# Seven products for eight in the A12 B21 term of gate and up, and table look-ups shared between VectorE and ScalarE

## The chip, the cores and the metric

The kernel runs on one core of one Trainium2 chip. The metric is the device time of that core in microseconds (us). Before the change three runs gave 1091.67, 1090.79 and 1091.09 us; their median is 1091.09 us. The core has a matrix engine (TensorE, PE in the profile; its weight loads are PEld), a vector engine (VectorE, DVE), an activation engine (ScalarE, ACT), a general engine (GpSimd, POOL), which here only issues transfers, and SyncE (SP), which issues most transfers. Each engine works through its own queue in order.

## What is computed

The input x has the shape 2 x 2048 x 512, float32. The reference is one pre-normed block of a transformer:

```python
x = x + attention(layernorm(x), Wq, Wk, Wv, Wo)
x = x + ffn(layernorm(x), lut, gate_idx, up_idx, down_idx)

def attention(x, Wq, Wk, Wv, Wo):      # between channels: 512 x 512 per batch element
    q, k, v = x @ Wq, x @ Wk, x @ Wv
    weights = softmax(q.T @ k / sqrt(16))
    return (weights @ v.T).T @ Wo

def ffn(x, lut, gate_idx, up_idx, down_idx):
    gate = x @ lut[gate_idx].T         # gate_idx, up_idx: 1376 x 512, values 0 to 15
    up = x @ lut[up_idx].T
    return (silu(gate) * up) @ lut[down_idx].T     # down_idx: 512 x 1376
```

The weights of the feed-forward part are not given as numbers but as indices into a table `lut` of 16 float32 values. So they have to be looked up, 3 x 1376 x 512 entries in all, before TensorE can use them.

## The kernel before the change

The 4096 tokens are handled as 8 chunks of 512 tokens (`NCH`), each of 4 blocks of 128 (`J`). The inner size 1376 is cut into 11 tiles of 128 rows, the last of 96 (`FT`, `NFT`). All products are in float32, in which one matmul of the code, 128x128 by 128x512, becomes two PE instructions in the profile. The program runs in stages, one after the other on TensorE:

- the Gram stage (`gram`, L427): normalizes x and multiplies it with itself for each batch element, block by block;
- the squares (`Square`, L580): small 512x512 products that turn the Gram matrix and the attention weights into one matrix m per batch element, with the softmax between them;
- the attention output (the loop at the end of which line 841 stands): for each of 32 blocks k it transposes a stored block on VectorE (`n_turned`, L734), multiplies it by m (`y_product`, L739), adds it to x and takes the statistics of the second layernorm (`added`, L747, with ScalarE doing a square and a sum), and normalizes the block six behind on ScalarE (`f_normed`, L757), which also issues a store of it every second block. The stored blocks are loaded again by GpSimd's queue and transposed by VectorE 16 blocks later;
- gate and up (`GateUp`, L860), in 44 units (f, p): tile f of the weights, pair p of chunks (1024 tokens);
- down (`Down`), with stores of the result.

Gate and up are multiplied together, by Strassen's scheme in Winograd's form: with gate weights A11, A12 on top and up weights A21, A22 below (A11 is two blocks of 128 wide along the contracted axis, and so are the others), and two chunks of tokens as B's columns, seven products replace eight. Each product of a unit is two matmuls, so a unit has 14. `Line.run` (L927) writes the order of a unit by hand: a1, c1, then the previous unit's last product a4, then a2, c2, b (which is A12 B21) and a3. After each of these seven stages it calls `between` (L962). The products a1, a2, a3 and a4 accumulate one after the other in one PSUM bank, and c1 and c2 in another. Between two of them ScalarE copies the intermediate sum out (p, p7 and u2, at L884, L890 and L895), VectorE adds (c2, b, a3), and ScalarE applies silu to the two halves of the result (h0 after b, h1 after a4). The next product into the bank has to wait for such a copy.

The look-ups are `Job`s (L236). A job fetches indices by a DMA from GpSimd's queue, ScalarE casts them to int16 (`cast`, L247), and VectorE does everything else (`ops`, L255): it makes three bit masks and one full-width mask out of the lowest bit, makes 8 choices between neighbouring table entries (L275), and then 7 choices by the other three bits with `copy_predicated` (L287). A gate-and-up job does both matrices of one f at once, 1024 entries per partition, followed by four sums for Strassen's scheme (`after`).

The look-ups have no place of their own: all jobs form one generator (`looked_up`, L350), and `pump(us)` (L367) draws operations from it where the hand-written order has room. Each operation yields a cost in us, and `pump` keeps what is owed:

```python
def pump(us):
    owed[0] = min(owed[0] + us, 2 * us + 1.0)
    while owed[0] > 0:
        cost = next(lookup, None)
        if cost is None:
            return
        owed[0] -= cost
```

A job whose gate is shut (its weight buffer is still in use) yields None; what is owed then stays. `between` pumps 1.0, or takes one operation out of the list `todo` in place of it. Line 841 pumps 1.4 for each of the first 16 blocks of the attention output and 0.7 for each of the others. In the Gram stage and the squares the pumps add up to 22.4 and 32.0.

Of the kernel before, what the change touches and what calls it, by code (L numbers as in the profile page):

```python
# [63 lines left out]
def tile_attn_ffn(  # L65
# [45 lines left out]
    eps_sb = const.tile([P, 1], F32, tag="eps", name="eps_sb")  # L111
    lut_i = lut_sb.bitcast(I32)
# [11 lines left out]
    wgu = tc.alloc_tile_pool(name="wgu", bufs=2)  # L124
# [111 lines left out]
    class Job:  # L236
        def __init__(self, name, rows, cols, load, dest, after, gate):
            self.name, self.rows, self.cols = name, rows, cols
            self.load, self.dest, self.after, self.gate = load, dest, after, gate

        def fetch(self, queue=nc.gpsimd):
            self.idx = gub.tile([P, 1024], I32, tag="idx", name=f"idx_{self.name}", bufs=2)[
                : self.rows, : self.cols
            ]
            self.load(queue, self.idx)
# [5 lines left out]
        def bits(self, tag, bufs):  # L251
            t = gub.tile([P, 1024], I16, tag=tag, name=f"{tag}_{self.name}", bufs=bufs)
            return t[: self.rows, : self.cols]

        def ops(self):  # L255

            rows, f, idx, b3 = self.rows, self.cols / 1024, self.idx, self.b3
            vec = nc.vector
            w = self.dest()
            b1, b2 = self.bits("b1", 1), self.bits("b2", 1)  # L260
            vec.tensor_scalar(b1, b3, 2, None, ALU.bitwise_and)
            vec.tensor_scalar(b2, b3, 4, None, ALU.bitwise_and)
            yield 0.2 + 0.54 * f

            vec.tensor_scalar(idx, idx, 31, 31, ALU.logical_shift_left, ALU.arith_shift_right)
            yield 0.1 + 0.55 * f
            vec.tensor_scalar(b3, b3, 8, None, ALU.bitwise_and)
            yield 0.1 + 0.27 * f
            masks = [None, b1, b2, b3]

            def pick(level, at, dest):

                if level == 1:
                    k = at // 2
                    vec.tensor_scalar(  # L275
                        dest.bitcast(I32), idx, lut_x[:rows, k : k + 1],
                        lut_i[:rows, at : at + 1], ALU.bitwise_and, ALU.bitwise_xor,
                    )
                    yield 0.2 + 0.55 * f
                    return  # L280
                yield from pick(level - 1, at, dest)
                half = 1 << (level - 1)
                t = gub.tile(
                    [P, 1024], F32, tag="pick", name=f"{self.name}_{level}_{at}", bufs=3
                )[:rows, : self.cols]
                yield from pick(level - 1, at + half, t)
                vec.copy_predicated(dest, masks[level - 1], t)  # L287
                yield 0.1 + 1.17 * f

            yield from pick(4, 0, w)  # L290
            yield from self.after()

    gu = {}
    passed = [0]

    def gu_job(f):
        f0, rows = FT[f]
        n = KB * rows

        def load(queue, idx):  # L300
            queue.dma_start(idx[:, :n], gate_idx[:, KB * f0 : KB * f0 + n])
            queue.dma_start(idx[:, n:], up_idx[:, KB * f0 : KB * f0 + n])

        def dest():
            gu[f] = {
                "w": wgu.tile([P, 2, KB, P], F32, tag="w", name=f"w_{f}"),
                "s": wgu.tile([P, 3, 2, P], F32, tag="s", name=f"s_{f}"),
            }
            flat = gu[f]["w"].rearrange("p g k r -> p (g k r)")[:, : 2 * n]
            gu[f]["flat"] = flat  # L310
            return flat

        def after():
            flat = gu[f]["flat"].rearrange("p (g k r) -> p g k r", g=2, k=KB)
            a11, a12 = flat[:, 0, 0:2, :], flat[:, 0, 2:4, :]
            a21, a22 = flat[:, 1, 0:2, :], flat[:, 1, 2:4, :]
            s1, s2, s4 = (gu[f]["s"][:, q, :, :rows] for q in range(3))
            for op, d, u, v in (
                (add, s1, a21, a22), (sub, s2, s1, a11), (sub, a21, a11, a21), (sub, s4, a12, s2)
            ):  # L320
                op(d, u, v)
                yield 0.42
            gu[f].update(
                {"11": a11, "12": a12, "S3": a21, "22": a22, "S1": s1, "S2": s2, "S4": s4}
            )

        return Job(f"gu{f}", P, 2 * n, load, dest, after, lambda: f < 2 + passed[0])

    def down_job(i, n=1):

        f0, rows = FT[i]

        def load(queue, idx):
            queue.dma_start(
                idx.rearrange("p (o e) -> p o e", o=n),
                down_idx[f0 : f0 + n * rows, :].rearrange("(o p) e -> p o e", o=n),
            )

        def dest():
            return wd[:rows, i : i + n, :].rearrange("p o e -> p (o e)")  # L340

        return Job(f"wd{i}", rows, n * E, load, dest, lambda: iter(()), lambda: True)


    jobs = [gu_job(0), gu_job(1), down_job(0, 2), down_job(2, 2), down_job(4), gu_job(2)]
    for i in range(5, NFT):
        jobs += [gu_job(i - 2), down_job(i)]
    jobs += [gu_job(f) for f in range(NFT - 2, NFT)]

    def looked_up():  # L350

        for i, job in enumerate(jobs):
# [4 lines left out]
            for k, cost in enumerate(job.ops()):  # L357
                yield cost
                if k == 9 and i + 1 < len(jobs):
                    jobs[i + 1].cast()  # L360
# [167 lines left out]
    for c in range(1, NCH):  # L528
        for j in range(J):
# [19 lines left out]
            if c == 1 and j == 2:  # L549
                nc.vector.tensor_tensor(  # L550
                    lut_x, lut_pairs[:, :, 0], lut_pairs[:, :, 1], ALU.bitwise_xor
                )
            if c == CPB and j == 1:
                gram_out(0)
# [274 lines left out]
    for k in range(NBLK):  # L829
# [11 lines left out]
        pump(1.4 if k < LAG else 0.7)  # L841
# [7 lines left out]
    def psum(tag, name):  # L849
        return fps.tile([P, E], F32, tag=tag, name=name, bufs=2)  # L850
# [8 lines left out]

    class GateUp:  # L860


        def __init__(self, f, p):
            self.f, self.p, self.rows = f, p, FT[f][1]
            self.name = f"{f}_{p}"

# [30 lines left out]
        def c2(self):  # L897
            mm(self.c, self.pairs("22", "T4"), False)
            self.c21 = self.temp("c21")
            add(self.c21, self.c, self.u2)  # L900

        def b(self):
            b = self.view("b")
            mm(b, self.pairs("12", "21"), True)
            self.h0 = self.temp("h0", 2)
            add(self.h0, b, self.p1)
            nc.scalar.activation(self.h0, self.h0, AF.Silu)  # L907
# [6 lines left out]
        def first(self):  # L914
            nc.vector.tensor_tensor(self.h0, self.h0, self.c21, ALU.mult)
            self.store(self.h0, 2 * self.p)

        def a4(self):
            mm(self.a, self.pairs("S4", "22"), False)
            self.h1 = self.temp("h1", 2)  # L920
# [6 lines left out]
    class Line:  # L927
# [5 lines left out]
        def run(self, u, final=False):  # L933
# [3 lines left out]
            self.between()  # L937
            last, self.last = self.last, u
# [4 lines left out]
            self.between()  # L943
            u.c2()
# [17 lines left out]
    def between():  # L962
        if todo:
            todo.pop(0)()
        else:
# [82 lines left out]
    class Down:  # L1048
# [94 lines left out]

        def end(self):
# [13 lines left out]
    for f, p in units:  # L1158
        while "S4" not in gu[f]:
            next(lookup)  # L1160
        assert p in xs
        if f == NFT - 1 and p == 0:
            assert not todo and next(lookup, None) is None
            xnp.release()
# [7 lines left out]
            todo += by_two(down_sums(hps["dT"]))  # L1172
# [6 lines left out]
        if p == NPR - 1:  # L1179
            passed[0] = f + 1  # L1180

# [83 lines left out]
```

## Time and profile before

| | us |
|---|---|
| median of three runs | 1091.09 |
| time of the profiled execution | 1091.32 |
| its span on the core | 1089.1 |
| TensorE busy | 1081.1 |
| VectorE busy | 712.3 |
| ScalarE busy | 321.4 |
| GpSimd busy | 33.4 |

The profile is of one execution. Its rows of slices cut the span into 40 equal parts of about 27 us, and each digit is the busy share of a slice in tenths. A row of a group of instructions names line, engine, operation, output and input, shape and count; behind the bar stand the total busy time in us, the mean of one in ns, and the idle time of the engine just before them with what ended it. "PE a_g L855" is a matmul of gate and up, in bank a. TensorE's granted clock was 1.00 in all the stretches looked at. The chain of work that ended last is TensorE for 92% of the span, ScalarE and VectorE for 3% each.

### The profile page before, as it was taken

Reading aid. Unit: us, or ns where it says so; the run is one execution under the profiler, and the core shown is the slowest. Engines: PE = TensorE matmul, PEld = TensorE weight load, DVE = VectorE, ACT = ScalarE, POOL = GpSimd, SP = SyncE. Lnnn points to the kernel's source line nnn. Section 1 sums busy time; section 2 is a strip of 40 time slices with the busy share of each in tenths; the row PEclk is TensorE's granted clock in tenths of the full one; section 3 lists DMA queues with packets and bytes.
Section 4 is the critical chain, followed back from the end, with each engine's and each line's share of the span. In section 5 each row is a group of like instructions: output and inputs, shape, how many; then the busy total and the mean of one; then the engine's idle time right before and its main releaser. Section 6 shows DMA issues by size and latency. Waiting matters only on the chain.

```text
span 1089.1 us, 10098 instructions
## 1 busy us (share of the span) xinstructions
PE 1081.1 (99%) x3458; PEld 647.9 (59%) x3458; DVE 712.3 (65%) x1357; ACT 321.4 (30%) x586; POOL 33.4 (3%) x66
## 2 busy tenths in 40 slices
PE   8999999999999999999999999999999999999998
PEld 5668886444444444444444444444338888888887
DVE  7878777887685787788878787763653334433341
ACT  4652532555622222222222222222222111111110
POOL 0000000112100000000000000000000000000000
PEclk9999999999999999999999999999999999999999
DMA  8650313697651111111121111111415554345421
GB/s 343 220 191 21 77 39 88 156 230 203 168 141 39 58 67 50 58 58 68 48 68 67 56 58 54 48 49 39 147 49 177 172 152 155 101 146 179 154 68 39
DMA packets 87699, 117.13 MB, mean 108 GB/s; under 512 B 14160, under 2 KB 50256, under 8 KB 86752
## 3 DMA queue, kind: packets, MB, share of 16 engines
q1 hardware_dynamic: 62784, 83.91, 24.4%
q0 software_dynamic: 4800, 15.80, 5.8%
q10 hardware_dynamic: 20064, 16.78, 4.8%
q8 instruction: 27, 0.44, 0.2%
q14 instruction: 24, 0.20, 0.1%
HBM read 68.76 MB, written 47.71 MB: 107 GB/s over the span
## 4 chain that ended last, share of the span: by engine, by line
PE 92%; ACT 3%; DVE 3%; ACTq 1%; DMA 1%; issue 1%; SPq 0%; DVEq 0%
PE a_g L855 28%; PE a_d L855 14%; PE c_g L855 14%; PE y L743 10%; PE c_d L855 7%; PE b_g L855 7%; PE b_d L855 4%; PE ea_t L580 1%; PE ea_p L580 1%; PE ea_m L580 1%; ACT xn_a L229 1%; PE gp L427 1%; ACT n L229 1%; DMA x<-in_x_dram 1%; DVE st_a L151 1%
## 5 line engine op out<-in xcount | busy, mean ns | idle before, releaser
L743 PE MATMUL y<-m,nT 128*128 128x512 f32 x256 | 110.2, 592 | 0.0
L133 DVE TENSOR_TENSOR c<-c_g,u 128x512 f32<-128x512 f32 (+1 forms) x44 | 30.4, 691 | 114.3 <-PE c_g L855 114.3
L743 PEld LDWEIGHTS y<-m,nT 128*128 128x128 f32 x256 | 48.6, 190 | 60.4 <-issue 58.6
L855 PE MATMUL c_g<-xb,w 128*128 128x512 f32 (+1 forms) x176 | 82.7, 592 | 0.0
L855 PE MATMUL a_g<-xT_a,s 128*128 128x512 f32 (+1 forms) x176 | 82.7, 592 | 0.0
L855 PE MATMUL a_g<-xb,w 128*128 128x512 f32 (+1 forms) x176 | 82.7, 592 | 0.0
L855 PE MATMUL b_g<-xb,w 128*128 128x512 f32 (+1 forms) x176 | 82.7, 592 | 0.0
L855 PE MATMUL a_g<-xb,s 128*128 128x512 f32 (+1 forms) x176 | 82.7, 592 | 0.0
L907 ACT ACTIVATE h<-h 128x512 f32<-128x512 f32 (+1 forms) x44 | 27.7, 630 | 163.2 <-DVE h L133 163.2
L427 PE MATMUL gp<-xn_a 128*128 128x128 f32 (+3 forms) x256 | 70.3, 435 | 2.7 <-DVE xn_a L174 1.6
L855 PE MATMUL a_g<-xT_sq,s 128*128 128x512 f32 (+1 forms) x132 | 62.0, 592 | 0.0
L427 PEld LDWEIGHTS gp<-xn_a 128*128 128x128 f32 x256 | 43.9, 190 | 29.6 <-issue 15.1
L275 DVE TENSOR_SCALAR gu<-idx_gu,lut_x,lut_sb 128x1024 int32<-128x1024 int32 (+1 forms) x77 | 58.4, 791 | 0.0
L855 PEld LDWEIGHTS a_g<-xb,s 128*128 128x128 f32 (+1 forms) x176 | 33.0, 188 | 42.6 <-issue 38.2
L855 PEld LDWEIGHTS a_g<-xT_a,s 128*128 128x128 f32 (+1 forms) x176 | 33.0, 188 | 42.5 <-issue 42.5
L855 PEld LDWEIGHTS b_g<-xb,w 128*128 128x128 f32 (+1 forms) x176 | 33.0, 188 | 42.5 <-issue 42.5
L855 PEld LDWEIGHTS c_g<-xb,w 128*128 128x128 f32 (+1 forms) x176 | 33.0, 188 | 42.5 <-issue 42.3
L855 PEld LDWEIGHTS a_g<-xb,w 128*128 128x128 f32 (+1 forms) x176 | 33.0, 188 | 42.5 <-issue 42.5
L287 DVE COPY_PREDICATED gu<-b_gu,gu 128x1024 f32<-128x1024 int16 (+1 forms) x44 | 56.4, 1281 | 0.8
L855 PE MATMUL a_d<-dT,hs_a 128*128 128x256 f32 x224 | 56.2, 378 | 0.0
L287 DVE COPY_PREDICATED wd<-b_wd,wd 128x512 f32<-128x512 int16 (+2 forms) x63 | 54.1, 859 | 1.1
L884 ACT COPY p<-a_g 128x512 f32<-128x512 f32 (+1 forms) x44 | 25.8, 586 | 78.0 <-PE a_g L855 78.0
(246 smaller groups left out, 1751.0 us busy)
## 6 DMA issues: line engine op xcount, KB each, us to landing
hd<-h SPq DMA_DIRECT2D x80, 256.0 KB, 2.0
h<-hd SPq DMA_DIRECT2D x40, 512.0 KB, 6.6
nl<-nd SPq DMA_DIRECT2D x32, 256.0 KB, 5.6
xnd<-xn_f ACTq DMA_DIRECT2D x16, 512.0 KB, 5.9
fl<-xnd POOLq DMA_DIRECT2D x32, 256.0 KB, 6.2
xn_back<-xnd SPq DMA_DIRECT2D x32, 256.0 KB, 3.7
out_dram<-r SPq DMA_DIRECT2D x31, 256.0 KB, 2.9
x<-in_x_dram SPq DMA_DIRECT2D x7, 1024.0 KB, 14.0
```

The source lines that it names most:

```text
L133: nc.vector.tensor_tensor(dest, a, b, ALU.add)
L151: nc.vector.bn_stats(st, block)
L229: nc.scalar.activation(to, block, AF.Identity, bias=self.nmr[:, j : j + 1], scale=self.rstd[:, j : j + 1],)
L275: vec.tensor_scalar(dest.bitcast(I32), idx, lut_x[:rows, k : k + 1], lut_i[:rows, at : at + 1], ALU.bitwise_and, ALU.bitwise_xor,)
L287: vec.copy_predicated(dest, masks[level - 1], t)
L427: nc.tensor.matmul(gp[b][i][:, i * P :], xn[:, i, j % 2, :], xn[:, i:, j % 2, :], start=c % CPB == 0 and j == 0, stop=c % CPB == CPB - 1 a ...
L580: nc.tensor.matmul(ps[:, m, :], self.a[a][:, k, m * P : (m + 1) * P], self.b[b][:, k, :], start=first and m == k == 0, stop=k == 1, skip_g ...
L743: nc.tensor.matmul(ys[k], nTs[k][:, i, :], m[:, i, :], start=(i == 0), stop=(i == KB - 1))
L855: nc.tensor.matmul(ps, lhsT, rhs, start=first and i == 0, stop=i == len(pairs) - 1, skip_group_check=not first,)
L884: nc.scalar.copy(self.p1, self.a)
L907: nc.scalar.activation(self.h0, self.h0, AF.Silu)
```

## The change

It has two parts.

**Products.** For f = 2 to 9, the four units made by two neighbouring f and two neighbouring p (a "group") share the term A12 B21. Seen over the group this is a product of 2x2 blocks, and it is done by the seven products of the same scheme, one matmul each, in place of eight. Each unit has a role, 0 to 3. Role 0 does two of the products, role 1 three (two of them in the new calls `extra1` and `extra2`, which come after c1 and after a2), role 2 two (one in `extra1`), role 3 none. They accumulate in two new single banks, x and y; two intermediate sums (r5, r6) are kept in SBUF by ScalarE copies. New sums of blocks are made on VectorE: `l2_sums` once per two pairs, `l2_left` for each two f. For f = 10 two blocks of B are already overwritten, so b uses two other sums there. c2's sum is now made in u2's place.

**Look-ups.** All jobs are 512 entries wide: gate and up are separate. The first six jobs of the list (`SHARED = 6`) are done by VectorE as before. In the other 27 the choice by the lowest bit is ScalarE's: b0 is 0 or 1, and an ACTIVATE with a per-partition scale and bias gives entry + b0 x (next entry - entry) for one 16-bit half of the table entry, as an integer, written to every second 16 bits of the result. So each of the 8 choices takes two ACTIVATEs, and no full-width mask is needed. The gates of the jobs change: a gate job may run up to 3 tiles ahead of the last f whose units have all been written out, an up job 2 tiles ahead of the last f whose a4 has been. The costs that the new job yields are written in the code below. The pumps of the attention output go from 1.4 and 0.7 to 1.6 and 1.0, and `between` pumps 0.3 beside an operation of `todo`.

```diff
...
         def ops(self):
+            return self.shared_ops() if self.scalar else self.vector_ops()
+
+        def shared_ops(self):
+
+
+            rows, f, b3 = self.rows, self.cols / 1024, self.b3
+            vec = nc.vector
+            w = self.dest()
+            b0, b1, b2 = self.bits("b0", 1), self.bits("b1", 1), self.bits("b2", 1)
+
+            def by_bit0(at, dest):
+                d = dest.bitcast(I16).rearrange("p (c h) -> p c h", h=2)
+                for h in range(2):
+                    nc.scalar.activation(
+                        d[:, :, h], b0, AF.Identity, bias=lut_h[:rows, at, h : h + 1],
+                        scale=lut_d[:rows, at // 2, h : h + 1],
+                    )
+
+            def temp(tag, bufs=1):
+                t = gub.tile([P, 512], F32, tag=tag, name=f"{tag}_{self.name}", bufs=bufs)
+                return t[:rows, : self.cols]
+
+            def both(mask, dest, t):
+                vec.copy_predicated(dest, mask, t)
+                return 0.15 + 1.17 * f
+
+            vec.tensor_scalar(b0, b3, 1, None, ALU.bitwise_and)
+            vec.tensor_scalar(b1, b3, 2, None, ALU.bitwise_and)
+            by_bit0(0, w)
+            t0 = temp("k1", 2)
+            by_bit0(2, t0)
+            yield 0.54
+            vec.tensor_scalar(b2, b3, 4, None, ALU.bitwise_and)
+            vec.tensor_scalar(b3, b3, 8, None, ALU.bitwise_and)
+            t4, t6 = temp("k2"), temp("k1", 2)
+            by_bit0(4, t4)
+            by_bit0(6, t6)
+            yield 0.54
+            t8 = temp("k3")
+            by_bit0(8, t8)
+            yield both(b1, w, t0)
+            t10 = temp("k1", 2)
+            by_bit0(10, t10)
+            yield both(b1, t4, t6)
+            yield both(b2, w, t4)
+            t12 = temp("k2")
+            by_bit0(12, t12)
+            t14 = temp("k1", 2)
+            by_bit0(14, t14)
+            yield both(b1, t8, t10)
+            yield both(b1, t12, t14)
+            yield both(b2, t8, t12)
+            yield both(b3, w, t8)
+            yield from self.after()
+
...
+        return Job(f"g{f}", P, n, load, dest, after, lambda: f < 3 + passed[0])
...
+        def after():
+            g, u = gw[f], up[0].rearrange("p (k r) -> p k r", k=KB)
+            t = wgu.tile([P, 3, 2, P], F32, tag="s", name=f"s_{f}", bufs=2)
+            a11, a12, a21, a22 = g[:, 0:2, :], g[:, 2:4, :], u[:, 0:2, :], u[:, 2:4, :]
+            s1, s2, s4 = (t[:, q, :, :rows] for q in range(3))
+            for op, d, v, w in (
                 (add, s1, a21, a22), (sub, s2, s1, a11), (sub, a21, a11, a21), (sub, s4, a12, s2)
             ):
-                op(d, u, v)
+                op(d, v, w)
                 yield 0.42
-            gu[f].update(
-                {"11": a11, "12": a12, "S3": a21, "22": a22, "S1": s1, "S2": s2, "S4": s4}
-            )
-
-        return Job(f"gu{f}", P, 2 * n, load, dest, after, lambda: f < 2 + passed[0])
-
-    def down_job(i, n=1):
-
+            gu[f] = {"11": a11, "12": a12, "S3": a21, "22": a22, "S1": s1, "S2": s2, "S4": s4}
+        return Job(f"u{f}", P, n, load, dest, after, lambda: f < 2 + ended[0])
...
+    SHARED = 6
+
+    jobs = [job(f) for f in range(2) for job in (gate_job, up_job)]
+    jobs += [down_job(i) for i in range(6)]
+    for f in range(2, NFT - 1, 2):
+        jobs += [gate_job(f), up_job(f), gate_job(f + 1), up_job(f + 1), down_job(5 + f // 2)]
+    jobs += [gate_job(NFT - 1), up_job(NFT - 1), down_job(NFT - 1)]
+    assert len(jobs) == 3 * NFT
+    for job in jobs[SHARED:]:
+        job.scalar = True
...
-                if k == 9 and i + 1 < len(jobs):
+                if k == (5 if job.scalar else 9) and i + 1 < len(jobs):
                     jobs[i + 1].cast()
...
-        pump(1.4 if k < LAG else 0.7)
+        pump(1.6 if k < LAG else 1.0)
...
+    def l2_sums(g):
+
+        x11, x21 = xb[4 * g][:, 2, :], xb[4 * g][:, 3, :]
+        x12, x22 = xb[4 * g + 2][:, 2, :], xb[4 * g + 2][:, 3, :]
+        t = x2p.tile([P, 3, CH], F32, tag=f"l{g}", name=f"l2b_{g}")
+        t1, t2, t4 = (t[:, q, :] for q in range(3))
+        l2b[g] = {"11": x11, "21": x21, "22": x22, "T1": t1, "T2": t2, "T3": x12, "T4": t4}
+        return [
+            lambda: sub(t1, x12, x11), lambda: sub(t2, x22, t1),
+            lambda: sub(x12, x22, x12), lambda: sub(t4, x21, t2),
+        ]
...
+        a11, a12 = gw[f][:, 2, :], gw[f][:, 3, :]
+        a21, a22 = gw[f + 1][:, 2, :], gw[f + 1][:, 3, :]
+        s1, s2, s3, s4 = (t[:, q, :] for q in range(4))
+        l2a[f // 2] = {"22": a22, "S1": s1, "S2": s2, "S3": s3, "S4": s4}
+        return [
+            lambda: add(s1, a21, a22), lambda: sub(s2, s1, a11),
+            lambda: sub(s3, a11, a21), lambda: sub(s4, a12, s2),
+        ]
...
+            self.role = 2 * (f % 2) + p % 2 if 1 < f < NFT - 1 else None
...
-            self.c21 = self.temp("c21")
-            add(self.c21, self.c, self.u2)
+            add(self.u2, self.c, self.u2)
+        def extra1(self):
+            if self.role == 1:
+                mm(two["x"], self.pair("S2", "T2"), False)
+                two["r6", self.p // 2] = r6 = self.kept("r6")
+                nc.scalar.copy(r6, two["x"])
+            elif self.role == 2:
+                two["y"] = self.view("y")
+                mm(two["y"], self.pair("S3", "T3"), True)
+                r5 = two["r5", self.p // 2]
+                add(r5, two["y"], r5)
+
+        def extra2(self):
+            if self.role == 1:
+                mm(two["x"], self.pair("S1", "T1"), False)
+                two["r5", self.p // 2] = r5 = self.kept("r5")
+                nc.scalar.copy(r5, two["x"])
...
+            elif self.role == 0:
+                two["x"] = self.view("x")
+                mm(two["x"], [(gw[self.f][:, 2, :], l2b[g]["11"])], True)
+                b = self.view("b")
+                mm(b, [(gw[self.f][:, 3, :], l2b[g]["21"])], True)
+                add(h0, two["x"], self.p1)
+                add(h0, b, h0)
+            elif self.role == 1:
+                mm(two["x"], self.pair("S4", "22"), False)
+                add(h0, two["x"], self.p1)
+            elif self.role == 2:
+                mm(two["y"], self.pair("22", "T4"), False)
+                add(h0, two["r6", g], self.p1)
+                add(h0, two["y"], h0)
+            else:
+                add(h0, two["r5", g], self.p1)
+            nc.scalar.activation(h0, h0, AF.Silu)
...
         def a4(self):
             mm(self.a, self.pairs("S4", "22"), False)
+            if self.p == NPR - 1:
+                ended[0] = self.f + 1
...
             u.c1()
             self.between()
+            u.extra1()
             last, self.last = self.last, u
             if last is not None:
                 last.a4()
                 self.between()
             u.a2()
             self.between()
+            u.extra2()
             u.c2()
...
     def between():
         if todo:
             todo.pop(0)()
+            pump(0.3)
         else:
             pump(1.0)
...
-        while "S4" not in gu[f]:
+        while f not in gu or f > 1 and min(f + 1, NFT - 1) not in whole:
             next(lookup)
         assert p in xs
+        if 1 < f < NFT - 1 and f % 2 == 0 and p == 0:
+            todo += l2_left(f)
...
+        if f == 1 and p % 2:
+            todo += l2_sums(p // 2)
```

## The prediction

> **What bounds the kernel now.** I read the page's busy shares and slices first, then busy times by stretch, the chain, the cost of single instructions, and ScalarE's (ACT's) timeline in one unit.
>
> ```profile
> span 1089.1 us, 10098 instructions
> PE 1081.1 (99%) x3458; PEld 647.9 (59%) x3458; DVE 712.3 (65%) x1357; ACT 321.4 (30%) x586; POOL 33.4 (3%) x66
> PE   8999999999999999999999999999999999999998
> DVE  7878777887685787788878787763653334433341
> ACT  4652532555622222222222222222222111111110
> ```
>
> TensorE (PE) never rests. VectorE (DVE) is at 7 to 8 tenths until slice 26, ACT at 2 in the gate-and-up stage but 5 to 6 in the stage before it (slices 7 to 10). Busy times of four stretches (the second to fifth figures are PE, PEld, DVE, ACT):
>
> ```profile
> 192.00:232.00 40.00, 40.00 (x94) 17.67 (x93) 33.30 (x82) 22.77 (x52) 5.59 (x10) 1.00 0.76 183
> 232.00:275.00 43.00, 43.00 (x102) 19.00 (x101) 33.73 (x84) 22.25 (x53) 7.66 (x14) 1.00 0.84 217
> 289.75:819.00 529.25, 529.25 (x1242) 232.58 (x1242) 389.30 (x618) 149.21 (x246) 15.07 (x28) 1.00 0.20 66
> 395.16:407.18 12.02, 12.02 (x30) 5.32 (x28) 10.59 (x14) 2.99 (x5) 1.08 (x2) 1.00 0.26 88
> ```
>
> The first two lie in the attention output ("y"), the third is all of gate and up, the fourth one unit (f, p) of it. The chain in that unit is PE alone:
>
> ```profile
> 395.32 1.72 PE c_g L855 x4
> 397.04 3.43 PE a_g L855 x8
> 400.48 1.72 PE c_g L855 x4
> 402.19 1.72 PE b_g L855 x4
> 403.91 3.43 PE a_g L855 x8
> ```
>
> A product of two 128-row blocks takes 1.72 us (four PE instructions), so one matmul of the code takes 0.86, and a unit 14 x 0.86 = 12.02. What ACT does meanwhile:
>
> ```profile
> 395.42 0.59 ACT L884 COPY p<-a_g 128x512 f32<-128x512 f32 x1 [0.89 <-PE a_g L855]
> 397.12 0.59 ACT L890 COPY p<-c_g 128x512 f32<-128x512 f32 x1 [1.12 <-PE c_g L855]
> 398.80 0.60 ACT L921 ACTIVATE h<-a_g 128x512 f32<-128x512 f32 x1 [1.09 <-PE a_g L855]
> 400.57 0.59 ACT L895 COPY u<-a_g 128x512 f32<-128x512 f32 x1 [1.17 <-PE a_g L855]
> 404.67 0.63 ACT L907 ACTIVATE h<-h 128x512 f32<-128x512 f32 x1 [3.52 <-DVE h L133]
> ```
>
> Each copy empties a bank that PE accumulates into again two stages (3.43 us) after it is filled. So a copy may start 3.43 - 0.59 = 2.8 us late; any later and PE stands.
>
> **The change, part by part.** *Products.* Units with f = 2 to 9 form 8 groups of four. A12 B21 costs a group's four units 2, 3, 2 and 0 matmuls, 7 for 8: 8 x 0.86 = **6.9 us less** on PE, all on the path. New sums on DVE: three adds of 0.68 per group, four 128-column sums per pair of f, eight 512-wide sums once: 8 x 2.0 + 4 x about 1 + 5.5 = 26 us; two ACT copies per group, 8 x 1.2 us.
>
> *Look-ups, DVE.* A 512-wide look-up costs DVE now (rows below) 8 x 0.54 + 7 x 0.73 + about 1.2 = 10.6 us, afterwards 7 x 0.73 + 4 x 0.28 = 6.2. Over 27 of them, most cheaper per entry now since 1024 wide, DVE loses some 80 us. That is worth nothing by itself: PE's waits on DVE add up to a few us in the trace. It does cover the new sums, VectorE's in-place sum into u2 and the moved table preparation (two small operations more), all costed at nothing (without it a unit's DVE, 10.6 of 12.0 us, would be nearly full). The u copy now also waits for the unit before it to have multiplied u2 away, 5 stages earlier: nothing, unless DVE lags by some 6 us (then the lag, at most). The index loads halve and double in number on POOL's queue, where they land 3 us after issue and are wanted about 7 us later: nothing.
>
> *Look-ups, ACT.* Each of 27 look-ups issues 16 ACTIVATEs of 128x512 with two per-partition operands, and a cast.
>
> ```profile
> L222 ACT ACTIVATE r<-xn_back,nmr_a,rstd_a 128x512 f32<-128x512 f32 x32 | 24.7, 809 | 33.4 <-DMA xn_back<-xnd 33.4
> L249 ACT CAST b_gu<-idx_gu 128x1024 int16<-128x1024 int32 x10 | 10.4, 1042 | 0.6 <-ACT n L229 0.6
> L249 ACT CAST b_wd<-idx_wd 128x512 int16<-128x512 int32 x6 | 3.6, 602 | 0.0
> L275 DVE TENSOR_SCALAR wd<-idx_wd,lut_x,lut_sb 128x512 int32<-128x512 int32 x48 | 24.0, 537 | 0.0
> L287 DVE COPY_PREDICATED wd<-b_wd,wd 128x512 f32<-128x512 int16 x42 | 30.7, 730 | 0.8
> ```
>
> The nearest row is L222: 0.81 alone, and the timeline shows two of them in 1.52, a step of 0.71. A look-up is then 16 x 0.71 + 0.5 = 11.9 us of ACT. All 27 come to 320 us, which ACT's 30% has room for; whether each stage has room is the question.
>
> The trace has no ACTIVATE that reads 16 bits or writes every second 16 bits. From below: the skill's "ScalarE: Activation LUTs", section "What ACT_TABLE_LOAD costs", gives one element per cycle for 2-byte and 4-byte types alike; the casts, (1042 - 602)/512 = 0.86 ns an entry with int16 results, agree on the output side. A doubled rate on 16 bits, which only the page excludes for inputs, would give 0.71 - 0.21 = 0.50. From above, a doubled time per entry gives 1.14; "SBUF — State Buffer", section "Door 1: The DMA port swizzle", lets eight 2-byte entries' stride pass free, and here it is two. I take 0.71.
>
> *The pace.* pump hands out look-ups by DVE costs: 0.54 for a step with four ACTIVATEs, 0.735 for the rest, 6.2 per look-up. ACT's time is not in it. The new ACTIVATEs wait for DVE's masks and for temporaries that DVE frees; behind them on ACT's in-order queue stand the copies of p, p7 and u, and PE waits for those.
>
> *Stage y.* Pumped before y: 22.4 (Gram) + 32.0 (squares) = 54.4. Jobs of 9.8, 11.4, 9.8, 11.4, 9.7, 9.7 leave 7.2 of the last VectorE job, gone after 4.5 blocks of 3.43 us at 1.6. So the next 11.6 blocks (about 192 to 232) hold three shared look-ups: ACT 22.8 + 3 x 11.9 = 58.5 in 40 us; at 1.0 two more (to 275): 22.3 + 23.8 = 46 in 43; DMA issues on ACT (0.52 every second block, not counted busy) add 6. Excess 28, less about 3 of slack: **+25 us**. PE feels it through DVE: copy_predicated waits for ACT, and the transposes that PE reads stand behind it.
>
> *Gate and up.* 22 look-ups remain, opened per f by gates. While the gate is shut, owed grows to 3.0; the first open pump comes after a4 (5.15 into a unit) and issues five steps with 12 ACTIVATEs, 8.5 us, ahead of the u copy. I followed one odd f by hand, in emission order, with 0.71 for ACT, 0.62 for DVE steps:
> - First unit, times from its start, with the extra matmul after c1: product a4 ends at 6.0, silu of h1 at 6.6. The burst (12 x 0.71) runs to 15.1, copy u to 15.6. Undisturbed, a3 starts at 10.3: it is 5.3 late.
> - The next pump (owed 0.7) issues t12 and t14, to 18.4, then the cast, 18.9. DVE's two copy_predicated on them (19.7) stand ahead of its two h0 adds (21.0); ACT's silu waits for those, idle for 2.1; copy p ends at 22.2.
> - The up half's four S sums and the next look-up's masks on DVE end at 24.6: ACT idle again. Its four ACTIVATEs end at 27.4 and copy p7 at 28.0, where PE's c2 was ready at 25.8.
> - The next two pumps put 6 + 2 ACTIVATEs and a silu ahead of the next copy u: 28.0 + 8 x 0.71 + 2 x 0.5 = 34.6. The second unit's a3 was due at 20.6: 14 late. What is left of the look-up falls behind that copy and within the slack, and the gate shuts.
>
> An odd f thus costs **14**. An even f has three look-ups, but the four queued l2 sums hold owed to 1.6 at the first burst: 10 ACTIVATEs, to 12.9, u at 13.4, +3.1. In its second unit a pump at owed 0.995 issues eight ahead of the r5 copy, which ends at 29.7; b needs it and was ready at 25.4 (itself 3 late): with a3 behind it the unit ends at 32.3 instead of 24.9, 7.4 late. In the third unit eight more stand ahead of u (38.0 to 43.7, u at 44.2): **+9**. f = 1 and 9, with more pumps of 0.3 or a narrower tile, have shorter bursts: 8 and 9, an estimate from the two worked. Sum 4 x 9 + 3 x 14 + 8 + 9 = **+95**.
>
> Total: 1091.3 (the profiled execution; its span 1089.1, 2.2 around it, median 1091.1) - 6.9 + 25 + 95 = **1204**. The down stage stays.
>
> **Rivals.** *Throughput only (0.22).* If ACT and DVE hand over without idle time, ACT just runs full. Odd f: 32 x 0.71 + 1 + 8 copies x 0.51 = 27.8 in 18.9 us, less slack 2.9: 6. Even: 7.8 - 2.9 = 4.9. With f = 1 and 9 some 44; y 21 without the waits at job ends: 1091 - 7 + 44 + 21 = **1150**. For it: semaphores may be met earlier than in my hand order. Against: the row of silu on h already waits 3.5 us for DVE in one unit.
>
> *Faster (0.07).* 16-bit ACTIVATEs run so cheaply that copies stay within their slack: **1084**. It decides at the u copy: 12 ACTIVATEs must fit into 10.3 - 0.5 - 6.6 = 3.2 us, 0.27 each; at 0.40, y's 48 would fit too and the bursts' rest roughly eats the 6.9. Below 0.4 it is a gain. Against it: no 128x512 row of ACT is under 0.56.
>
> *Dearer writes (0.07).* 1.14 each: 0.43 x 430 = 186 more, nearly all exposed: about **1390**.
>
> *The product isn't saved or its gain and the stalls cancel (0.02):* 1091.
>
> **How the numbers follow.** Main case 0.62, its own range 1170 to 1235. For 8 in 10 the range goes down into the throughput case, 1130, and up to 1240. Faster by over 0.2% (2 us, about what a measurement tells from no change) 0.07, within 0.02, slower 0.91.
>
> **What would show it.** PE's idle time in stage y and in gate and up, released by "ACT u", "ACT p" or DVE; ACT's slices at 8 to 9 there; PE busy down by 7 us; the new ACTIVATE's mean near 0.8 (step 0.71). Right in kind but small: idle only behind bursts. Wrong: a mean under 0.5, or DVE's row still the releaser with ACT idle.

## The result and the profile after

The changed kernel takes 1288.22 us (median of four runs, 1287.02 to 1290.02), the kernel before 1091.12: a ratio of 1.1807, with a 95% interval from 1.1792 to 1.1821. The forecast was 1204 in a range from 1130 to 1240. Its direction was right; the loss is 197 us where 113 were forecast (198 us by the spans of the two profiled executions, which are used from here on). The profiled execution took 1289.2 us, with a span of 1287.4. From its page, in the order of the lines shown of before, with TensorE's granted clock added:

```profile
span 1287.4 us, 10567 instructions
PE 1137.1 (88%) x3442; PEld 659.3 (51%) x3442; DVE 674.0 (52%) x1440; ACT 667.0 (52%) x1047; POOL 35.2 (3%) x70
PE   9999997588998787597959796879789999999998
DVE  7788785477765444445444454444446344444441
ACT  4633329888428676838683877487642221111110
PEclk9999999899998998798989898889899999999999
```

Three things are to be seen. TensorE has gaps in slices 6 to 29 (counted from 0), the stretch in which ScalarE is mostly at 6 to 9; where ScalarE falls to 2 to 4 there, TensorE is at 8 or 9. ScalarE's busy time doubled, as it had to, but its share of the whole span is only 52%: the average hides the stages. And TensorE was busy for 56 us *longer* (1137.1 against 1081.1) with 16 instructions *less*; the clock row has digits below 9 only in slices that have gaps. The two stages that changed, y and then gate and up (PE, PEld, DVE and ACT are the second to fifth figures; the clock is the third from the end):

```profile
174.60:324.30 149.70, 120.57 (x266) 50.72 (x265) 95.99 (x239) 120.07 (x214) 16.79 (x31) 0.94 0.56 139
324.30:1018.60 694.30, 580.26 (x1237) 245.81 (x1236) 342.07 (x628) 431.56 (x623) 14.89 (x28) 0.91 0.16 52
```

From the same marks (first y product, first product of gate and up, first of down) the stages took 111.6 and 533.1 us before. Stage y is 38.1 longer: TensorE idle for 149.7 - 120.6 = 29.1, and 120.6 - 111.6 = 9.0 of slower work. Gate and up are 161.2 longer: idle for 694.3 - 580.3 = 114.0, and 580.3 - (533.1 - 6.9) = 54.1 of slower work, less the 6.9 us of matmuls saved. The rest differs by 1 us. So 143 us are idle time and 63 are slow matmuls; less the 6.9 saved and that 1, they make the 198. Who TensorE waited for (time in total, times, longest):

```profile
PE a_g L969 <- ACT u L1013: 70.1, 15, 7.4
PE y L824 <- DVE nT L808: 29.1, 14, 6.0
PE a_g L969 <- ACT p L1002: 15.7, 4, 6.5
PE x_g L969 <- ACT r L1042: 15.0, 3, 5.0
```

Nearly always the releaser in gate and up is a ScalarE copy (all but 2.1 us, which are waits for a VectorE sum). In y it is VectorE's transpose, and that stands behind VectorE's own wait for ScalarE, as here ahead of a wait of 5.95 us, one of y's two longest:

```profile
231.78 0.73 DVE L285 COPY_PREDICATED k_wd<-b_wd,k_wd 128x512 f32<-128x512 int16 x1 [4.11 <-ACT k_wd L275]
232.41 0.70 DVE L808 STREAM_TRANSPOSE nT<-nl 128x512 f32<-128x512 f32 x1
```

The stretch that the prediction worked out by hand, an odd f (here f = 5), on ScalarE:

```profile
643.72 0.60 ACT L1088 ACTIVATE h<-a_g 128x512 f32<-128x512 f32 x1 [1.95 <-PE a_g L969]
644.21 1.76 ACT L275 ACTIVATE wu<-b_u,lut_h,lut_d 128x512 int16<-128x512 int16 x2
645.83 8.18 ACT L275 ACTIVATE k_u<-b_u,lut_h,lut_d 128x512 int16<-128x512 int16 x10
653.85 0.59 ACT L1013 COPY u<-a_g 128x512 f32<-128x512 f32 x1
...
664.13 1.76 ACT L275 ACTIVATE wg<-b_g,lut_h,lut_d 128x512 int16<-128x512 int16 x2 [2.38 <-DVE b_g L288]
```

The burst of twelve, the copy u behind it and the later idle wait for VectorE's masks are all there. TensorE in the same stretch:

```profile
646.95 1.02 PE L969 MATMUL y_g<-l2b,wg 128*128 128x512 f32 x2
654.49 3.78 PE L969 MATMUL a_g<-xT_sq,s 128*128 128x512 f32 x4 [6.52 <-ACT u L1013]
658.06 2.65 PE L969 MATMUL a_g<-xb,wg 128*128 128x512 f32 x4
660.55 1.88 PE L969 MATMUL c_g<-xb,wu 128*128 128x512 f32 x4
...
675.36 3.78 PE L969 MATMUL a_g<-xT_a,s 128*128 128x512 f32 x4 [5.40 <-ACT u L1013]
```

The idle times 6.52, then 2.11 (before c2, not shown) and 5.40 add up to 14.0, the same figure as the hand working's for an odd f (a section below comes back to that). What it didn't have is in the durations: after the first wait two stages take 660.55 - 654.49 = 6.06 us in place of 3.43, after the last one the first four instructions take 3.78 in place of 1.88.

### The profile page after: what moved, and what is told of

It is laid out like the page before. It is cut to its first block, busy times and chain, and to the rows that moved or that the text cites. A ratio compares the mean times of both kernels' runs of the same rounds, so it can differ in the third digit from the quotient of the medians.

```text
span 1287.4 us, 10567 instructions
## 1 busy us (share of the span) xinstructions
PE 1137.1 (88%) x3442; PEld 659.3 (51%) x3442; DVE 674.0 (52%) x1440; ACT 667.0 (52%) x1047; POOL 35.2 (3%) x70
## 4 chain that ended last, share of the span: by engine, by line
PE 61%; ACT 27%; DVE 7%; issue 3%; ACTq 1%; DMA 1%; SPq 0%; DVEq 0%
PE a_g L969 20%; PE a_d L969 12%; PE c_g L969 8%; ACT k_wd L275 6%; PE c_d L969 6%; ACT k_u L275 6%; ACT k_g L275 6%; PE b_d L969 3%; PE y L824 2%; PE x_g L969 1%; PE b_g L969 1%; ACT wd L275 1%; ACT wu L275 1%; PE ea_t L661 1%; PE ea_p L661 1%
## 5 line engine op out<-in xcount | busy, mean ns | idle before, releaser
L824 PE MATMUL y<-m,nT 128*128 128x512 f32 x256 | 119.1, 620 | 29.1 <-DVE nT L808 29.1
L275 ACT ACTIVATE k_wd<-b_wd,lut_h,lut_d 128x512 int16<-128x512 int16 (+1 forms) x126 | 105.5, 940 | 2.6 <-ACT xn_f L233 2.4
L275 ACT ACTIVATE k_g<-b_g,lut_h,lut_d 128x512 int16<-128x512 int16 (+1 forms) x126 | 103.5, 924 | 1.2 <-ACT xn_f L233 0.6
L275 ACT ACTIVATE k_u<-b_u,lut_h,lut_d 128x512 int16<-128x512 int16 (+1 forms) x126 | 102.4, 925 | 0.0
L137 DVE TENSOR_TENSOR u<-c_g,u 128x512 f32<-128x512 f32 (+1 forms) x44 | 30.3, 688 | 124.1 <-PE c_g L969 105.3
L969 PE MATMUL a_g<-xb,wg 128*128 128x512 f32 (+1 forms) x176 | 93.1, 655 | 0.0
L969 PE MATMUL c_g<-xb,wu 128*128 128x512 f32 (+1 forms) x176 | 82.7, 592 | 0.0
L969 PEld LDWEIGHTS a_g<-xb,wg 128*128 128x128 f32 (+1 forms) x176 | 39.9, 226 | 57.4 <-issue 57.4
L969 PEld LDWEIGHTS a_g<-xT_sq,s 128*128 128x128 f32 (+1 forms) x132 | 27.0, 211 | 81.1 <-ACT u L1013 49.8
L285 DVE COPY_PREDICATED k_wd<-b_wd,k_wd 128x512 f32<-128x512 int16 (+1 forms) x36 | 26.0, 732 | 55.8 <-ACT k_wd L275 32.6
L969 PEld LDWEIGHTS c_g<-xb,wu 128*128 128x128 f32 (+1 forms) x176 | 33.0, 188 | 42.8 <-issue 42.6
```

Of the source, the lines that this page charges most:

```text
L137: nc.vector.tensor_tensor(dest, a, b, ALU.add)
L275: nc.scalar.activation(d[:, :, h], b0, AF.Identity, bias=lut_h[:rows, at, h : h + 1], scale=lut_d[:rows, at // 2, h : h + 1],)
L285: vec.copy_predicated(dest, mask, t)
L824: nc.tensor.matmul(ys[k], nTs[k][:, i, :], m[:, i, :], start=(i == 0), stop=(i == KB - 1))
L969: nc.tensor.matmul(ps, lhsT, rhs, start=first and i == 0, stop=i == len(pairs) - 1, skip_group_check=not first,)
```

## The experiments

What was expected of each, with a rival, stands ahead of its result. The ratios are to the kernel before, at 1091.1 to 1091.4 us.

**Taking the change apart.** Four kernels each undo one part. The first leaves all look-ups to VectorE:

```diff
-    SHARED = 6
+    SHARED = 33
```

> The changed kernel with all 33 look-ups left to VectorE (512 wide); the seven products stay. Main theory (the loss is all ScalarE's look-ups, the products are worth their eight matmuls): 1091.1 - 6.9 = 1084.2 us, TensorE's clock 1.00. Rival (the new sums and VectorE's 512-wide look-ups fill VectorE, so TensorE waits for it): 1090 us or more, with waits of PE for DVE in gate and up.

Measured: 1100.13 us, ratio 1.0087 (1.0074 to 1.0099). The rival was right here. The clock is 0.995 and ScalarE no longer a releaser, but VectorE is:

```profile
PE a_g L969 <- DVE c L137: 7.5, 4, 2.5
PE y_g L969 <- DVE r L137: 2.9, 1, 2.9
```

So the part that the prediction costed at nothing, because VectorE's relief covers it, costs 16 us against the forecast 1084 once that relief is gone. The runs under "What the products are worth" look for where.

The second keeps the shared look-ups and does A12 B21 with eight products, without the extra sums:

```diff
-            self.role = 2 * (f % 2) + p % 2 if 1 < f < NFT - 1 else None
+            self.role = None
```

> The changed kernel with A12 B21 done by eight products as before, and none of the extra sums; the shared look-ups stay. Main theory: the two parts add up, so 1288 + 7 = 1295 us, within 8 (the stalls keep their places). Rival (the extra matmuls, banks and copies r5 and r6 of the products cause a good part of the stalls): 1270 or less.

Measured: 1293.91 us, 1.1857 (1.1839 to 1.1875). The look-ups alone make the whole loss; the products take 5.7 us off in their company.

The third and the fourth share the look-ups of one stage only:

```diff
-    for job in jobs[SHARED:]:
+    for job in jobs[SHARED:11]:      # third: five, in y
+    for job in jobs[11:]:            # fourth: 22, in gate and up
```

> The changed kernel, but only the five look-ups of the attention output are shared with ScalarE; the 22 of gate and up are VectorE's. Main theory: that stage alone costs its 38 us over before (149.7 against 111.6), so 1084 + 38 = 1122 us. Rival (lateness of one stage is made up in the next, or a stall in it delays later ones): off this by over 10.

> The opposite: the 22 look-ups of gate and up are shared, the five of the attention output are VectorE's. Main theory: 1288 - 38 = 1250 us, with gate and up at 694 us as in the changed kernel. Rival as in the run before: off this by over 10.

Measured: 1138.91 us, 1.0436 (1.0422 to 1.0450), and 1250.47, 1.1459 (1.1444 to 1.1475). The fourth is as expected. The third misses 1122 by 17, more than the 10 that its rival named. But 1122 was built on 1084 for the rest, and with all look-ups on VectorE that rest measured 1100, and the third is 38.8 above it. Stage y takes 149.7 us in it (174.2 to 323.9), as in the changed kernel, and gate and up take 692.9 in the fourth (286.2 to 979.1) for 694.3, so neither stage acts much on the other. So y's loss adds to either: 1100.1 + 38.8 = 1138.9, and 1250.5 + 38 = 1288.

**What a wait costs TensorE.** To see the slow matmuls by themselves, three kernels take the kernel before and delay the u copy in the 32 units with f = 2 to 9, with needless ScalarE copies:

```diff
+            if 1 < self.f < NFT - 1:
+                for i in range(10):          # second and third: 16
+                    nc.scalar.copy(self.temp("late"), self.p7)
             nc.scalar.copy(self.u2, self.a)
...
         def a3(self):
+            if 1 < self.f < NFT - 1:         # third only
+                spare = fps.tile([P, E], F32, tag="spare", name=f"spare_{self.name}", bufs=1)
+                for i in range(3):
+                    mm(spare, self.pairs("11", "11"), True)
             mm(self.a, self.pairs("S1", "T1"), False)
```

> The kernel before, with ten needless ScalarE copies of 128x512 ahead of the u copy in each of the 32 units with f = 2 to 9: the copy then ends about 10 x 0.49 later, 2.1 us behind what the slack of 2.8 us covers. Main theory (short waits cost TensorE only their length, as after the waits of 2.1 us and less in the changed kernel's trace, where four matmuls took 1.98 us instead of 1.88): 1091 + 32 x 2.1 = 1158 us, or up to 1165. Rival (any wait costs as much again in slow matmuls): 1220 or more.

> The same with sixteen copies, so a wait of 16 x 0.49 - 2.8 = 5.0 us in each of 32 units. Main theory (a wait this long is followed by matmuls at half rate, about 2 to 2.6 us lost each time): 1091 + 32 x (5.0 + 2.3) = 1325 us, with TensorE's clock below 0.95. Rival (a wait costs its length): 1251.

> The same sixteen copies, and six needless matmuls of 128x512 into a spare bank just before a3, 5.15 us, so that TensorE works where it would wait. Nothing uses their result. Main theory (TensorE slows because it was idle): no slow matmuls are left, the clock is 1.00, and the time is 1091 + 32 x 5.15 = 1256 us, less than without the added matmuls. Rival (TensorE slows because of ScalarE's traffic or because of the copies themselves): the slow matmuls stay, 1325 or more.

Measured: 1207.16 us, 1.1065 (1.1047 to 1.1083); 1363.31, 1.2492 (1.2473 to 1.2511); 1300.46, 1.1917 (1.1899 to 1.1935). The copies into one tile follow each other at 0.64 us, not 0.49, so the waits are 2.38 and 6.27, and the last two times lie above the 1325 and 1256 expected. TensorE with ten copies, in two neighbouring units:

```profile
503.61 1.98 PE L855 MATMUL a_g<-xT_sq,s 128*128 128x512 f32 x4 [2.38 <-ACT u L898]
...
518.27 3.01 PE L855 MATMUL a_g<-xT_sq,s 128*128 128x512 f32 x4 [2.38 <-ACT u L898]
521.06 2.60 PE L855 MATMUL a_g<-xb,w 128*128 128x512 f32 x4
```

The same wait of 2.38 us is followed by full speed once and by matmuls near half rate the next time; that came after 18 of the 32 waits. With sixteen copies it comes after all 32:

```profile
502.22 3.78 PE L855 MATMUL a_g<-xT_a,s 128*128 128x512 f32 x4 [6.27 <-ACT u L898]
505.80 2.07 PE L855 MATMUL a_g<-xb,w 128*128 128x512 f32 x4
```

And with sixteen copies and matmuls in the gap:

```profile
503.81 4.45 PE L855 MATMUL spare<-xb,w 128*128 128x512 f32 x10
509.39 1.98 PE L855 MATMUL a_g<-xT_a,s 128*128 128x512 f32 x4 [1.12 <-ACT u L898]
```

By the spans (1204.2, 1361.7 and 1298.4 against 1089.1) and the idle times (32 waits: 76.0, 200.7, 36.0 us): ten copies, 115.1 - 76.0 = 39 us beyond the waits, 1.2 per wait, or 2.2 for each of the 18; sixteen, 272.6 - 200.7 = 72, 2.2 per wait; sixteen with 32 x 5.15 us of needless matmuls, 209.3 - 36.0 - 164.8 = 8.5, 0.3 per wait. The clock is 0.974, 0.920 and 1.000. ScalarE's delay is the same in the last two and TensorE has *more* to do in the last, which is yet 63 us faster. So it is being idle that slows TensorE, not ScalarE's traffic: that rival is out. The theory for short waits fell: the waits alone would have made 1091 + 76 = 1167, and each cost half as much again. What decides after which of these equal waits TensorE is slow, no run here settles. The Trainium skill, in "TensorE: Matmul & The Clock Gate", section "HAM oscillation — how this bites in real kernels", has the rule "no PE-idle gaps >~3.4µs", because the clock gate then halves the rate. Half rate is what the trace shows (3.78 for 1.88), but by the rule the ten copies would have ended at those 1167 us, and they measured 1207: a gap of 2.4 us isn't safe.

**What an ACTIVATE costs.** The next kernel writes the two halves side by side. Both take the same half of the table entry, so it computes with other weights:

```diff
-                d = dest.bitcast(I16).rearrange("p (c h) -> p c h", h=2)
+                d = dest.bitcast(I16).rearrange("p (h c) -> p c h", h=2)
...
-                        d[:, :, h], b0, AF.Identity, bias=lut_h[:rows, at, h : h + 1],
-                        scale=lut_d[:rows, at // 2, h : h + 1],
+                        d[:, :, h], b0, AF.Identity, bias=lut_h[:rows, at, 1:2],
+                        scale=lut_d[:rows, at // 2, 1:2],
```

> The changed kernel, but the two ACTIVATEs of a choice write their 16-bit results side by side, each into one half of the tile, instead of into every second 16 bits, and both write the upper half of the entry; so the looked-up weights have other values. Main theory (the stride of the write makes an ACTIVATE take 0.94 us instead of the 0.81 of float32): 0.81, 430 x 0.12 = 52 us less of ScalarE, most of it exposed and with less clock lost, about 1225 us. Rival (16-bit input is what costs): 0.94 and 1288 us again.

Measured: 1252.24 us, 1.1470 (1.1451 to 1.1489). The group in the changed kernel, and then with the results side by side:

```profile
L275 ACT ACTIVATE k_g<-b_g,lut_h,lut_d 128x512 int16<-128x512 int16 x112 | 93.9, 940 | 1.2 <-ACT xn_f L233 0.6 <-DVE nT L808 0.6
```

```profile
L275 ACT ACTIVATE k_g<-b_g,lut_h,lut_d 128x512 int16<-128x512 int16 x112 | 81.7, 804 | 1.3 <-ACT xn_f L233 0.6 <-DVE nT L808 0.6
```

The stride of the write is the difference in the instruction (besides the table column that scale and bias come from), 0.94 against 0.80; reading 16 bits costs nothing extra. It is worth 36 us of time, less than the 63 expected. The run has a second use: its ACTIVATEs cost what the prediction took (ten in 7.14 us, a step of 0.71). Its TensorE is idle for 19.1 us in y and 91.0 in gate and up, where the forecast had 25 and 95, and busy there for 698.0 where 111.6 + 526.2 were due: 60 us of slow matmuls.

**Bursts or amount.** One kernel charges the shared look-ups in ScalarE's time, and pumps more of it:

```diff
-            yield 0.54
+            yield 2.55          # four ACTIVATEs; 1.27 for two
...
-            pump(1.0)
+            pump(1.35)
```

> The changed kernel with the shared look-ups' costs in ScalarE's time (2.55 for four ACTIVATEs, 1.27 for two, at 0.64 of cost for one) and pumps of 1.35 in gate and up, so that no pump puts out more than about eight ACTIVATEs and most put out four. If bursts are the cause, most waits go: 1150 us or less. If the amount is (ScalarE needs 5 x 13.6 + 8 x 3 = 92 of 94 us in two f, and gates forbid an even spread), much stays: 1180 to 1260.

Measured: 1186.57 us, 1.0876 (1.0861 to 1.0891). This is in the range of "the amount", near its low end: the pace is worth 102 us, and 95 of the loss stay. Stage y has no loss left (gate and up start at 286.0), but look-ups have moved from it (ScalarE is busy there for 89.3 us, 120.1 in the changed kernel) to gate and up, where 612 us lie between the first and the last a1 products, 516 in the kernel before. By the estimate in the expectation ScalarE has 92 us of work for each 94 of TensorE's, which leaves little room for an even pace; that no other pace does better was not tried.

**What the products are worth.** The list of jobs is reordered, with all look-ups on VectorE, then with pumps of 1.1:

```diff
-        jobs += [gate_job(f), up_job(f), gate_job(f + 1), up_job(f + 1), down_job(5 + f // 2)]
+        jobs += [gate_job(f), up_job(f), gate_job(f + 1), down_job(5 + f // 2), up_job(f + 1)]
```

> The products with all look-ups on VectorE, and each group of five jobs in the order gate, up, gate, down, up, so that the down look-up falls into an odd f. Main theory (the 16 us over the forecast in the run with VectorE alone come from even f whose three look-ups, 30.9 by their own costs, don't fit into 25.9 of pumps and are then put out at once ahead of the next f's first unit): those waits go, and the time is 1084 to 1087 us. Rival (VectorE is too full in any order): 1095 or more.

> The same with 1.1 in place of 1.0 pumped after each stage of gate and up. Main theory (what still doesn't fit gets room): as the run before or up to 3 us less. Rival (more VectorE work per stage delays the sums that TensorE waits for): 3 us or more above the run before.

Measured: 1090.70 us, 1.0002 (0.9994 to 1.0010), and 1093.88, 1.0023 (1.0014 to 1.0032). The first lies between its two theories: 9 us better than 1100, but the products' gain is still gone. The waits left are in unit (3, 0), at the product that takes b's place, and just behind it (3.1 and 1.9 us, for VectorE). More pumping doesn't cure them: the second is 3.2 us above the first, as its rival had it, though the executions of either spread over some 3 us. The next kernel moves the down look-ups further, and gives two look-ups to ScalarE:

```diff
+    jobs += [gate_job(2), down_job(6), up_job(2)]
+    for f in range(3, NFT, 2):
+        jobs += [gate_job(f), up_job(f), gate_job(f + 1)]
+        jobs += [down_job(6 + f // 2), up_job(f + 1)]
+    for job in jobs[9:11]:
+        job.scalar = True
```

> The products, with all look-ups on VectorE but two (the down look-up 5 and the gate look-up 2, which fall to the end of the attention output and the first units, where pumps are 0.3 and ScalarE has room), and the down look-ups moved to where gates leave room: down 6 ahead of the first gate that shuts, the others after every second gate. By the costs no f is then overfull (21.2 for 25.9 where it was 30.9). Main theory (the products' 6.9 us are there once VectorE is never late): 1084 to 1087 us, clock 1.00. Rival (even two shared look-ups, or VectorE's fill, cost it again): 1090 or more.

Measured: 1096.88 us, 1.0049 (1.0036 to 1.0063). The rival again: the two shared look-ups cost their waits at the end of y and in the first units (the same order without them takes 1089.90, below). But its last wait is at 313 us; from f = 2 on TensorE waits for nothing. So the last two kernels keep that order without the last two lines of the diff, and the second pumps 0.6 instead of 0.3 beside an operation of `todo`:

> As the run with two shared look-ups, with the same order of jobs, but all look-ups on VectorE. Main theory (the 12 us were ScalarE's alone; the order is what clears gate and up, but f = 1 is again 2 to 3 short of pumps): 1084 to 1089 us. Rival (the two look-ups' VectorE work, 9.7 instead of 6.2 each, brings the waits at f = 2 and 3 back): 1090 or more.

> The same with 0.6 instead of 0.3 pumped beside an operation of the list: 8 more in the first 27 stages of gate and up, where VectorE is busy for 36 of 50 us in the kernel before. Main theory: nothing is put out at once any more, 1084 to 1086 us, 5 or more below before. Rival (VectorE, fuller there, is late with the sums that TensorE waits for): above the run before.

Measured: 1089.90 us, 0.9992 (0.9985 to 0.9998), and 1085.49, 0.9948 (0.9934 to 0.9961). The first is at the edge between its two theories, and waits for VectorE of 2.3 and 3.1 us at f = 2 are back, as its rival had it. The last is as expected, and beats both kernels. From its page, and its longest wait in gate and up:

```profile
PE 1075.7 (99%) x3442; PEld 644.5 (59%) x3442; DVE 768.2 (71%) x1656; ACT 330.8 (31%) x615; POOL 35.1 (3%) x70
```

```profile
PE c_g L966 <- DVE xb L134: 1.6, 1, 1.6
```

TensorE is busy for 5.4 us less than before, and 5.8 of the time are gained. It is the products that gain it: before the change TensorE had no wait in gate and up that an order of look-ups could have taken away. So the seven products are worth most of the 6.9 us that they save when VectorE is hardly ever late, and no look-up has to leave VectorE for that.

## Why the prediction was wrong

- **What bounds the kernel, and where the loss comes from**: right. TensorE's waits are at the copies named (u, p, p7, r5) and at VectorE's transposes in y, and the two stages add up, as the third and fourth kernels show.
- **The hand working of gate and up, +95**: the mechanism was right and its sum nearly so. Idle time is 114, and 91 at the price of an ACTIVATE that the working used. The match by f is partly luck: the 14.0 of f = 5 came with dearer ACTIVATEs, and at the working's own price f = 5 has 11.6 of idle time for 14, and f = 4 has 10.1 for 9. In the changed kernel f = 4 has 11.5, and f = 2, which was taken to be like it, 16.4.
- **Stage y, +25**: 29 idle (19 at that price), plus 9 of slow matmuls. So here too the dearer ACTIVATE hides a working that was somewhat too high.
- **"I take 0.71" for an ACTIVATE**: mis-sized, 0.82 in a row (8.18 for ten). The nearest row wrote 4-byte entries next to each other. The prediction had a bound from above, 1.14, and set it aside for the Trainium skill's sentence in "SBUF — State Buffer", section "Door 1: The DMA port swizzle", by which such a stride is free; for this write the measurement says otherwise. Worth 36 us of time, in part through the slow matmuls.
- **The step that failed is "the total": a wait was summed at its own length.** Before the change the clock was 1.00 throughout, and TensorE had no wait in gate and up that could show what follows one. The sum has a term for how long TensorE stands and none for how it runs afterwards. 63 us beside the idle time are matmuls that ran slowly after waits; a wait of 6.3 us was followed by 2.2 us of such loss, and the delayed copies in the kernel before show it by themselves, and the added matmuls take it away. With this term the forecast would have been 1204 + 63 = 1267, and with the measured idle time, 143 in place of 120, 1290. The measured idle time alone, without the slow matmuls, would have ended near 1225, inside the range. The price of an ACTIVATE didn't carry the time out: the kernel that writes side by side pays the forecast's price, has 110 us of idle time where 120 were forecast, and still takes 1252. The sign "PE busy down by 7 us" failed for the same reason: it went up by 56. No rival had the term either, and the trace of before couldn't show it.
- **Products, 6.9 us on the path**: nearly right as a size (5.7 beside the look-ups, 5.8 in the last kernel).
- **"All costed at nothing" for VectorE's new work**: nothing with the relief, as far as the runs show. Without it 16 us came. One down look-up of each two f, moved from the even to the odd one, took away 9 of them; a further order took 0.8 more and more room beside the queued sums 4.4. The relief itself was put at 80 us; VectorE's busy time fell by 38, with new sums in it that are put at 26, so by an estimated 64.
- **The case of throughput only (1150)**: out; ScalarE's idle waits for VectorE are in the timeline (2.38 us before the masks of the next look-up). The kernel paced in ScalarE's time is the nearest to it, and still at 1187.

## What to carry to other kernels

Work that is moved to an idle engine must be paced in that engine's time, and its amount weighed stage by stage: 52% busy on average was too much, because the copies that TensorE waits for stand in the same queue and have 2.8 us of slack. Pacing took back 102 of the 197 us. Where TensorE bounds a kernel, count a wait at more than its length: one of 6.3 us cost 2.2 more, one of 2.4 us 1.2 more on average, so these figures show no gain in cutting a long wait into short ones, while filling it with matmuls that nobody reads brought 1363 us down to 1300. Before a look-up is moved to another engine, try its order and its room on the engine where it is: here that took the kernel with the products from 1100 to 1085 us, where the move made it 1288.

## What the runs showed of the hardware

- TensorE idle for 2.4 us: after 18 of 32 waits it then ran slowly, 1.2 us lost on average and 2.2 for each of the 18. Idle for 6.3 us: after all 32, 2.2 lost each. Kept busy with matmuls that nobody reads (1.1 us of idle time left): clock 1.00.
- A ScalarE ACTIVATE of 128x512 that writes every second 16 bits: 0.94 us alone and 0.82 in a row; the same side by side 0.80 and 0.71. From the groups 384 and 512 wide: (940 - 791)/128 = 1.16 ns an entry with the stride.
- ScalarE copies of 128x512 from SBUF, all into one tile: 0.64 us apart, where two ACTIVATEs into different tiles, with two operands more, are 0.71 apart and the expectation had 0.49. Why, no run here settles.
